# Layer 1 attention of a two-layer model: wider score products, TensorE in a written order, key columns built on VectorE, expert rows fetched earlier

## The chip, the cores and the metric

The kernel runs on one core of one Trainium2 chip. The metric is the device time of one execution in microseconds (us). The time before is the median of three runs, 2395.29 us (2393.6 to 2425.56). The profile comes from one more execution, which took 2390.1 us and whose recorded span, first to last instruction, is 2388.3 us.

## The reference

The input is 32 sequences of 256 tokens with 128 features. Each of two layers adds attention(layernorm(x)) * silu(ffn(layernorm(x))) to x. Layer 0 is a product-of-scores attention with a mixture of eight experts. The change touches layer 1 alone: its attention, and the place where the results of its eight experts are fetched and weighted. Cut to that:

```python
def _strided_allowed(S):                      # STRIDE = 4, LOCAL = 8
    return (j % STRIDE == 0) | (jnp.abs(i - j) <= LOCAL)
...
q, k, v = x @ q_w, x @ k_w, x @ v_w           # 16 heads of 8
q = q * jax.nn.sigmoid(unity_scale)
scores = jnp.einsum('bhqd,bhkd->bhqk', q, k) / jnp.sqrt(D)
scores = jnp.where(_strided_allowed(S), scores, -jnp.inf)
out = jnp.einsum('bhqk,bhkd->bhqd', jax.nn.softmax(scores, axis=-1), v)
return out.reshape(B, S, H) @ o_w + o_b
...
# FFN: top-2 of 8 experts, a slot per token and choice, capacity limited
gathered = out[idx_k, loc_c]
y = jnp.einsum('tk,tkd->td', gates_k * valid, gathered)
```

## The kernel before, in words

The program runs in this order: layer 0, then layer 1's attention for the first half of the tokens (stage A), layer 1's experts (stage M), and layer 1's attention for the second half together with the combination of expert rows for all tokens (stage B). The 8192 tokens lie in 16 blocks of 512, and a block holds two sequences, so stages A and B have 16 sequences each.

**Attention.** A query may see every fourth key and the keys up to 8 places away. So for each block of 64 queries 124 key columns are picked: 64 strided ones and 60 near ones. Two blocks of 64 queries make a stack of 128 partitions; a sequence has two stacks. `prepare` makes one sequence ready: it transposes the normalised rows (`apst`), copies them to `axT`, gathers the key columns into `axk` (the strided ones on VectorE, L779; the near ones in four copies on GpSimd, L781), and multiplies for q, k and v (`apsq`, `apsk`, `apsv`). To keep the four heads that share 32 partitions apart, q is written four times into `aqm`, each time scaled by a mask that leaves one head (L788). The values go to `ava`, with a column of ones that GpSimd sets (L802).

`scores` takes two of the four groups of heads of one stack. Each group has one bank of PSUM (tag `psc`, four banks). A product with the identity first writes the mask of forbidden keys (L813), then 16 products of 32 rows by 64 columns and 124 keys add the scores (L821). VectorE takes the maximum (L828) and subtracts it (L829), ScalarE takes the exponential (L830). `values` transposes four heads (`apsT`, L835), ScalarE copies them to `apT` (L837), and 8 products per group (L842) give the weighted values, with the sum of the weights as a ninth column. `project` divides (L849, L851), transposes (`apso`), multiplies by the output weights (`apsf`) and adds the bias (L861).

The order on each engine comes from a list scheduler that works from its own estimate of times; engines work their queue in that order. `all` writes the rough order: the scores of one stack between the values of the stack before and the `prepare` of the next sequence.

**Moving rows.** In stage A the loop also sends rows to their expert slots: after each stack four indirect DMAs from GpSimd (L157, 128 in all). `pace` lets three start, then a small memset on GpSimd (`breath`, L141) waits for all three to land. Stage M reads these slots only when all have landed. In stage B `combine` fetches the two expert rows of each token of a block with eight indirect DMAs (L1022, 128 in all, paced in the same way), weights and adds them on VectorE (L1033, L1034), takes SiLU on ScalarE (L1036), multiplies by the attention (L1037) and adds x (L1038).

Of the kernel before, what the change touches and what calls it, by code (L numbers as in the profile page):

```python
# [11 lines left out]
F32 = mybir.dt.float32  # L12
# [8 lines left out]
P = 128  # L21
# [12 lines left out]
GROUP0 = (0, 14, 30, 44)  # L34
# [21 lines left out]
def model_kernel(ctx: ExitStack, tc: tile.TileContext, a: dict, out: bass.AP):  # L56
# [56 lines left out]
    qscale = const.tile([P, 4], F32, name="qscale")  # L113
# [106 lines left out]
    with ExitStack() as c0:  # L220
# [479 lines left out]
        us = w0.tile([P, 1], F32, name="us")  # L700
        nc.sync.dma_start(us, a["unity"].partition_broadcast(P))
        nc.scalar.activation(us, us, AF.Sigmoid)
        nc.vector.tensor_scalar(us, us, D ** -0.5, None, ALU.mult)
        nc.vector.tensor_scalar(qscale, hmask, us, None, ALU.mult)
# [49 lines left out]
    class Attention:  # L754

        def __init__(self, c, name, pairs):
            self.ak = c.enter_context(tc.tile_pool(name=f"ak{name}", bufs=2))
            self.pa = c.enter_context(tc.tile_pool(name=f"pa{name}", bufs=2, space=PSUM))  # L760
            self.pa1 = c.enter_context(tc.tile_pool(name=f"pb{name}", bufs=1, space=PSUM))
            self.seqs = [(p, b, dst) for p, dst in pairs for b in range(2)]
            self.steps = self.all()

        def pm(self, name):
            return self.pa1.tile([P, 512], F32, tag="pm", name=name)

        def prepare(self, p, b):
            ak = self.ak
            t0 = p * TT + 2 * b  # L770
            pst = self.pm("apst")
            for i in range(2):
                nc.tensor.transpose(pst[:, i * P : (i + 1) * P], xn[:, t0 + i, :], ident)
            xT = ak.tile([P, S], F32, tag="axT", name="axT")
            nc.scalar.copy(xT, pst[:, :S])

            xk = ak.tile([P, NQB, NK], F32, tag="axk", name="axk")
            grp = xT.rearrange("p (n f) -> p n f", f=4)
            nc.vector.tensor_copy(xk[:, :, 0:QB], bc(grp[:, :, 0], 1, NQB))  # L779
            for i in range(NQB):  # L780
                nc.gpsimd.tensor_copy(xk[:, i, QB:NK].rearrange("p (n f) -> p n f", f=3),  # L781
                                      grp[:, GROUP0[i] : GROUP0[i] + 20, 1:4])
            yield
            psq = self.pm("apsq")
            nc.tensor.matmul(psq[:, :S], lhsT=wqkvo[:, 0, :], rhs=xT, start=True, stop=True)  # L785
            qm = ak.tile([P, 4, S], F32, tag="aqm", name="aqm")
            for j in range(4):
                nc.scalar.activation(qm[:, j, :], psq[:, :S], AF.Copy, scale=qscale[:, j : j + 1])  # L788
            yield
            psk = self.pm("apsk")  # L790
            nc.tensor.matmul(psk[:, : NQB * NK], lhsT=wqkvo[:, 1, :],  # L791
                             rhs=xk.rearrange("p i k -> p (i k)"), start=True, stop=True)
            kT = ak.tile([P, NQB, NK], F32, tag="akT", name="akT")
            nc.scalar.copy(kT.rearrange("p i k -> p (i k)"), psk[:, : NQB * NK])
            yield
            psv = self.pm("apsv")
            for i in range(NQB):
                nc.tensor.matmul(psv[:NK, i * P : (i + 1) * P], lhsT=xk[:, i, :], rhs=wqkvo[:, 2, :],  # L798
                                 start=True, stop=True)

            va = ak.tile([P, NQB, NH, D + 1], F32, tag="ava", name="ava")
            nc.gpsimd.memset(va[:NK, :, :, D : D + 1], 1.0)  # L802
            for i in range(NQB):
                nc.vector.tensor_copy(va[:NK, i, :, 0:D],
                                      psv[:NK, i * P : (i + 1) * P].rearrange("k (h d) -> k h d", d=D))
            self.ready = qm, kT, va

        def scores(self, qm, kT, st, g, pr):

            views = []  # L810
            for w in range(2):
                sc = self.pa.tile([P, 512], F32, tag="psc", name="apsc", bufs=4)[:, : 4 * NK]
                nc.tensor.matmul(sc, lhsT=identb, rhs=keymask[:, st].rearrange("p j k -> p (j k)"),  # L813
                                 start=True, stop=False)
                views.append(sc)
            for u in range(2):
                i = 2 * st + u
                for j in range(4):
                    for w in range(2):
                        r = slice(32 * (g + w), 32 * (g + w) + 32)  # L820
                        nc.tensor.matmul(views[w][u * QB : (u + 1) * QB, j * NK : (j + 1) * NK],  # L821
                                         lhsT=qm[r, j, i * QB : (i + 1) * QB], rhs=kT[r, i, :],
                                         start=False, stop=(j == 3))
            for w in range(2):
                sv = views[w].rearrange("p (j k) -> p j k", j=4)
                to = pr[:, 4 * (g + w) : 4 * (g + w) + 4, :]
# [5 lines left out]
        def values(self, va, st, g, pr, avv):  # L832
            psT = self.pa.tile([P, 4, P], F32, tag="psT", name="apsT")
# [4 lines left out]
            yield  # L838
# [7 lines left out]
        def project(self, avv, dst):  # L846
# [6 lines left out]
            yield  # L853
            pso = self.pm("apso")
            nc.tensor.transpose(pso[:, :P], o, ident)  # L855
            oT = ak.tile([P, P], F32, tag="aoT", name="aoT")
            nc.scalar.copy(oT, pso[:, :P])
            yield
            psf = self.pm("apsf")
            nc.tensor.matmul(psf[:, :P], lhsT=oT, rhs=wqkvo[:, 3, :], start=True, stop=True)  # L860
            nc.vector.tensor_tensor(dst, psf[:, :P], ob, ALU.add)  # L861

        def stack_values(self, va, st, pr, dst):
            av = self.pa1.tile([P, 512], F32, tag="pav", name="apav")
            avv = av[:, : NH * (D + 1)].rearrange("p (h d) -> p h d", d=D + 1)
            for g in range(4):
                yield from self.values(va, st, g, pr, avv)
            yield from self.project(avv, dst)

        def all(self):  # L870

            for _ in self.prepare(*self.seqs[0][:2]):
                pass
            last = iter(())
            for n, (p, b, dst) in enumerate(self.seqs):
                qm, kT, va = self.ready
                if dst is None:
                    dst = self.late[p]
                ahead = iter(())
                for st in range(2):  # L880
                    pr = self.ak.tile([P, NH, NK], F32, tag="apr", name="apr")
                    if st and n + 1 < len(self.seqs):
                        ahead = self.prepare(*self.seqs[n + 1][:2])
                    for g in (0, 2):
                        self.scores(qm, kT, st, g, pr)
                        for _ in range(3):
                            next(last, None)
                            next(ahead, None)
                    for _ in last:
                        next(ahead, None)  # L890
                    for _ in ahead:
                        pass
                    last = self.stack_values(va, st, pr, dst[:, 2 * b + st, :])
                    yield
            for _ in last:
                pass
# [51 lines left out]
    with ExitStack() as ca:  # L948
# [11 lines left out]
        for _ in att.steps:  # L960
            dispatch1(4)
# [53 lines left out]
    with ExitStack() as cb:  # L1015
        bk = cb.enter_context(tc.tile_pool(name="bk", bufs=3))

        def combine(p, s):
# [10 lines left out]
            nc.sync.dma_start(x, x1[p])  # L1029
            y = bk.tile([P, TT, P], F32, tag="yc", name="yc")  # L1030
# [5 lines left out]
            nc.scalar.activation(y, y, AF.Silu)  # L1036
            nc.vector.tensor_tensor(y, y, s, ALU.mult)  # L1037
            nc.vector.tensor_tensor(y, y, x, ALU.add)  # L1038
            nc.sync.dma_start(outv[:, p * TT : (p + 1) * TT, :], y)

        late = range(NEARLY, NP)
        att = Attention(cb, "b", [(p, None) for p in late])
        att.late = {}
        steps = att.steps
        early = list(range(NEARLY))
        held = None
        for p in late:
            att.late[p] = bk.tile([P, TT, P], F32, tag="s1", name="s1")
            for _ in range(4):
                next(steps)  # L1050
            if early:
                q = early.pop(0)
                combine(q, sres[:, q * TT : (q + 1) * TT, :])
            if held is not None:
                combine(held, att.late[held])
            held = p
        for _ in steps:
            pass
        combine(held, att.late[held])


def _layout(i):
# [32 lines left out]
    for b in range(NQB):  # L1095
        keys = np.concatenate([
            np.arange(0, S, 4),
            (4 * (GROUP0[b] + np.arange(20))[:, None] + np.arange(1, 4)[None, :]).ravel(),
        ])
        query = b * QB + np.arange(QB)  # L1100
        allowed = (keys[None, :] % 4 == 0) | (np.abs(query[:, None] - keys[None, :]) <= 8)
        u = b % 2
# [48 lines left out]
```

## Time and profile before

| | us |
|---|---|
| median of three runs | 2395.29 |
| profiled execution | 2390.1 |
| its span | 2388.3 |
| first L781 copy of stage A | 1256.4 |
| first and last L157 row sent | 1286.1, 1538.5 |
| first transpose of stage M (L975) | 1697.1 |
| first and last L1022 row fetched | 1941.7, 2219.4 |

The last four rows, and every time of day in this document, count from the start of the span. Per engine the whole span holds 2153.5 us of matmuls on TensorE (90%), 1191.4 us on VectorE (50%), 990.7 us on ScalarE (41%) and 703.3 us on GpSimd (29%). Those are averages over stages with different limits; the change touches the span from 1255 us to 1697 us and from 1942 us to its end.

The L781 copies mark the sequences. In stage A they start at 1256.4, 1284.5, 1320.7, 1353.8, 1382.8, 1411.9, 1442.1, 1471.1, 1501.2, 1533.8 us and then at 1555.3, 1576.8, 1598.0, 1619.2, 1640.5, 1661.7 us. In stage B they start at 1942.7, 1957.6, 2001.6, 2030.9, 2068.8, 2104.1, 2141.8, 2170.9, 2197.1, 2220.4 us and then at 2238.7, 2261.4, 2287.1, 2307.7, 2328.6, 2349.9 us.

### The profile page before, as it was taken

To read this page: it belongs to the slowest core of one execution; us is meant where nothing else is said; L and a number is where in the kernel's file an instruction comes from. 1 tells how busy PE (TensorE), PEld (TensorE's weight loads), DVE (VectorE), ACT (ScalarE), POOL (GpSimd) and SP (SyncE) were. 2 spreads that over 40 slices of the span, in tenths; PEclk is the share of its full clock that TensorE was granted. 3 is DMA by queue.
4 is the path that set the end of the run, shared out by engine and by line. 5 is a ranking of instruction groups with operands and counts; after the bars stand their busy time and mean duration, and the time that the engine had idled before them with its cause. 6 is when DMAs were issued, how large, how long until landed. Compare 5 with 4: busy or idle time off the path is not lost. (4 is left out here: it accounts for less than half of the span.)

```text
span 2388.3 us, 51723 instructions
## 1 busy us (share of the span) xinstructions
PE 2153.5 (90%) x21618; PEld 1639.4 (69%) x21618; DVE 1191.4 (50%) x2610; ACT 990.7 (41%) x2041; POOL 703.3 (29%) x965
## 2 busy tenths in 40 slices
PE   6999999799999986866978888799999989989998
PEld 4776777588888864544756666577677767767776
DVE  6667666322222245755855444356433336445765
ACT  5523333244343333644742444355311125455654
POOL 0005555122222235555102555400000025444100
PEclk9989999899999987878986888799999977578999
DMA  8502111255454422222112111000122112121100
GB/s 260 178 8 75 43 44 34 85 172 154 149 173 153 148 99 76 80 74 70 44 43 96 33 37 35 25 2 2 55 73 72 64 53 58 50 56 46 36 6 11
DMA packets 131481, 177.19 MB, mean 74 GB/s; under 512 B 16304, under 2 KB 94659, under 8 KB 131248
## 3 DMA queue, kind: packets, MB, share of 16 engines
q1 hardware_dynamic: 103056, 96.57, 12.5%
q0 software_dynamic: 26752, 76.03, 10.7%
q8 instruction: 171, 2.80, 0.5%
q10 hardware_dynamic: 1440, 1.27, 0.2%
q14 instruction: 62, 0.51, 0.1%
HBM read 104.78 MB, written 69.21 MB: 73 GB/s over the span
## 5 line engine op out<-in xcount | busy, mean ns | idle before, releaser
L456 PE MATMUL pp<-qk 64*128 64x128 f32 x2048 | 210.8, 310 | 102.1 <-DVE pat L458 54.2
L441 ACT COPY qk<-ptr 128x512 f32<-128x512 f32 x256 | 149.2, 585 | 352.7 <-PE y L468 268.9
L456 PEld LDWEIGHTS pp<-qk 64*128 64x128 f32 x2048 | 148.9, 193 | 174.1 <-issue 124.8
L821 PE MATMUL apsc<-akT,aqm 32*64 32x124 f32 x4096 | 265.3, 293 | 0.0
L828 DVE TENSOR_REDUCE amx<-apsc 128x4 f32<-128x496 f32 x256 | 163.3, 669 | 190.5 <-PE apsc L821 190.4
L821 PEld LDWEIGHTS apsc<-akT,aqm 32*64 32x64 f32 x4096 | 206.8, 143 | 53.6 <-issue 46.8
L458 DVE TENSOR_TENSOR pat<-pp,dmask 128x512 f32<-128x512 f32 x256 | 175.5, 685 | 128.3 <-PE pp L456 127.0
L837 ACT COPY apT<-apsT 124x512 f32<-124x512 f32 x256 | 146.5, 587 | 177.8 <-PE apsT L835 176.6
L157 POOL DMA_INDIRECT disp<-xn,slot x128 | 136.6, 1067 | 222.3 <-DVE state L431 172.9
L835 PE MATMUL apsT<-ident,apr 128*124 128x128 f32 x1024 | 198.0, 308 | 0.0
L842 PEld LDWEIGHTS apav<-ava,apT 124*64 124x64 f32 x4096 | 152.1, 147 | 66.7 <-issue 29.3
L842 PE MATMUL apav<-ava,apT 124*64 124x9 f32 x4096 | 175.2, 212 | 4.9 <-ACT apT L837 3.0
L439 PE MATMUL ptr<-ident,feat 128*128 128x128 f32 x1024 | 171.0, 285 | 2.6 <-DVE feat L421 2.3
L607 DVE TENSOR_TENSOR od<-edn,wt 128x256 f32<-128x256 f32 x72 | 30.6, 425 | 285.2 <-PE edn L603 285.2
L596 ACT ACTIVATE ha<-eup,wt 128x256 f32<-128x256 f32 x288 | 119.2, 471 | 127.4 <-PE eup L591 124.6
L830 ACT ACTIVATE apr<-apr 128x496 f32<-128x496 f32 x256 | 152.8, 619 | 37.3 <-DVE apr L829 35.7
L829 DVE TENSOR_TENSOR apr<-apsc,amx 128x496 f32<-128x496 f32 x256 | 162.3, 665 | 0.6
L562 POOL DMA_INDIRECT wt<-in_wexp,wrow x72 | 69.0, 959 | 294.1 <-DVE xdT L584 261.3
L622 POOL DMA_INDIRECT rows<-moe,slot x128 | 134.3, 1049 | 65.5 <-issue 29.6
L439 PEld LDWEIGHTS ptr<-ident,feat 128*128 128x128 f32 x1024 | 120.1, 145 | 45.3 <-issue 38.2
L835 PEld LDWEIGHTS apsT<-ident,apr 128*124 128x124 f32 x1024 | 126.7, 152 | 32.2 <-issue 26.5
L802 POOL MEMSET ava<- 124x64 f32 x32 | 6.9, 223 | 478.6 <-DMA moe<-od 278.3
(211 smaller groups left out, 3937.5 us busy)
## 6 DMA issues: line engine op xcount, KB each, us to landing
disp<-zero SPq DMA_DIRECT2D x17, 1024.0 KB, 8.2
xd<-disp SPq DMA_DIRECT2D x72, 128.0 KB, 2.0
moe<-od SPq DMA_DIRECT2D x72, 128.0 KB, 2.0
x<-in_x SPq DMA_DIRECT2D x32, 256.0 KB, 3.3
part<-so SPq DMA_DIRECT2D x16, 512.0 KB, 2.9
soin<-part SPq DMA_DIRECT2D x16, 512.0 KB, 3.8
xd<-disp SPq DMA_DIRECT2D x32, 256.0 KB, 2.6
moe<-od SPq DMA_DIRECT2D x32, 256.0 KB, 2.0
```

Source lines behind the costliest of these rows:

```text
L157: ins = pace(lambda: nc.gpsimd.indirect_dma_start(out=self.dst[:, :], out_offset=bass.IndirectOffsetOnAxis(ap=idx, axis=0), in_=rows, in_o ...
L439: nc.tensor.transpose(pst[:, 2 * n + c], seq.feat[c][:, n, m * P : (m + 1) * P], ident)
L441: nc.scalar.copy(qk, pst)
L456: nc.tensor.matmul(psp[:, w, c], lhsT=qk[r, 2 + c], rhs=qk[r, c], start=True, stop=True)
L458: nc.vector.tensor_tensor(pat, psp, bc(bc(dmask, 1, 2), 1, 2), ALU.mult)
L821: nc.tensor.matmul(views[w][u * QB : (u + 1) * QB, j * NK : (j + 1) * NK], lhsT=qm[r, j, i * QB : (i + 1) * QB], rhs=kT[r, i, :], start=Fa ...
L828: nc.vector.tensor_reduce(mx, sv, AX.X, ALU.max)
L829: nc.vector.tensor_tensor(to, sv, bc(mx, 2, NK), ALU.subtract)
L830: nc.scalar.activation(to, to, AF.Exp)
L835: nc.tensor.transpose(psT[:NK, j, :], pr[:, 4 * g + j, :], ident)
L837: nc.scalar.copy(pT[:NK], psT[:NK])
L842: nc.tensor.matmul(avv[u * QB : (u + 1) * QB, h, :], lhsT=pT[:NK, j, u * QB : (u + 1) * QB], rhs=va[:NK, 2 * st + u, h, :], start=True, st ...
```

## The change

Layers 0 and the experts are left as they are. In layer 1's attention and in `combine`:

- The mask of a head moves from q to k. `qT` is one scaled copy; `kb` holds the keys four times, each with one head's rows left (two copies on ScalarE, two on VectorE). One product of 32 by 64 and 496 columns then gives four heads: eight products a stack in place of 32, and `scores` takes all four groups at once.
- The near keys become a regular window (20 groups of three, from 8 places before the block on), read with one strided VectorE copy from an `axT` that has zeros at both ends. Two fixed `axT` and two fixed `ava` are cleared once for each stage by GpSimd. The strided key columns are no longer copied: k and v are multiplied from `axT` directly.
- In stages A and B TensorE's instructions keep the order in which they are written; `stack` writes it. The other engines keep the list scheduler.
- The small PSUM tiles (`apst`, `apsq`, `apsk`, `apsv`, `apsT`, `apso`, `apsf`) share three banks; before, `apsT` had two and the others one.
- `combine` becomes a generator in three parts: fetch, weight and SiLU, multiply and store. A plan puts them at different stacks.

```diff
         def prepare(self, n):
...
-            xk = ak.tile([P, NQB, NK], F32, tag="axk", name="axk")
-            grp = xT.rearrange("p (n f) -> p n f", f=4)
-            nc.vector.tensor_copy(xk[:, :, 0:QB], bc(grp[:, :, 0], 1, NQB))
+            xT = self.xTs[n % 2]
+            nc.scalar.copy(xT[:, EDGE : EDGE + S], pst[:, :S])
+            strided = xT[:, EDGE : EDGE + S : 4]
+            xw = ak.tile([P, NQB, NK - QB], F32, tag="axw", name="axw")
+            nc.vector.tensor_copy(xw.rearrange("p i (n f) -> p i n f", f=3),
+                                  bass.AP(xT.tensor, xT[:, 1:].offset,
+                                          [xT[:, :].ap[0], [QB, NQB], [4, WG], [1, 3]]))
...
-            for j in range(4):
-                nc.scalar.activation(qm[:, j, :], psq[:, :S], AF.Copy, scale=qscale[:, j : j + 1])
+            nc.scalar.activation(qT, psq[:, :S], AF.Copy, scale=qscale)
...
+            nc.tensor.matmul(psk[:, :, :QB], lhsT=wqkvo[:, 1, :], rhs=bc(strided, 1, NQB),
+                             start=True, stop=True)
+            nc.tensor.matmul(psk[:, :, QB:], lhsT=wqkvo[:, 1, :], rhs=xw, start=True, stop=True)
+            kb = ak.tile([P, NQB, 4, NK], F32, tag="akb", name="akb")
+            for j in (0, 2):
+                nc.scalar.activation(kb[:, :, j, :], psk, AF.Copy, scale=hmask[:, j : j + 1])
+                nc.vector.tensor_scalar(kb[:, :, j + 1, :], psk, hmask[:, j + 1 : j + 2], None, ALU.mult)
...
-                nc.gpsimd.tensor_copy(xk[:, i, QB:NK].rearrange("p (n f) -> p n f", f=3),
-                                      grp[:, GROUP0[i] : GROUP0[i] + 20, 1:4])
...
         def scores(self, qT, kb, st, pr):
...
             for u in range(2):
                 i = 2 * st + u
-                for j in range(4):
-                    for w in range(2):
-                        r = slice(32 * (g + w), 32 * (g + w) + 32)
-                        nc.tensor.matmul(views[w][u * QB : (u + 1) * QB, j * NK : (j + 1) * NK],
-                                         lhsT=qm[r, j, i * QB : (i + 1) * QB], rhs=kT[r, i, :],
-                                         start=False, stop=(j == 3))
+                for g in range(4):
+                    r = slice(32 * g, 32 * g + 32)
+                    nc.tensor.matmul(views[g][u * QB : (u + 1) * QB, :],
+                                     lhsT=qT[r, i * QB : (i + 1) * QB],
+                                     rhs=kb[r, i].rearrange("p j k -> p (j k)"),
+                                     start=False, stop=True)
...
+        def stack(self, front, back, st, ahead, owed):
...
+            pT = {g: self.turn(g, pr) for g in range(2)}
+            if front is not None:
+                self.scores(*front)
+            between = ((ahead,), (owed,), (ahead,), (owed,)) if st == 0 else                 ((ahead,), (), (owed,), (owed, ahead))
+            for g in range(4):
+                self.values(va, sb, g, pT.pop(g), avv)
+                if g < 2:
+                    pT[g + 2] = self.turn(g + 2, pr)
+                for one in between[g]:
+                    next(one, None)
...
-        for _ in att.steps:
-            dispatch1(4)
+        with tc.manual_schedule(engines={mybir.EngineType.PE}):
+            for _ in att.steps:
+                dispatch1(4)
...
+        for n, p in enumerate(range(NEARLY, NP)):
+            plan += [(4 * n + t, p) for t in (2, 5, 6)]
+        for q in range(NEARLY):
+            plan += [(4 * q + t, q) for t in (0, 3, 3)]
```

## The prediction, made before the changed kernel ran

> **What bounds the kernel now.** I read the page first, then the busy time by stretch, the waits, and two stretches of the timeline.
>
> ```profile
> PE 2153.5 (90%) x21618; PEld 1639.4 (69%) x21618; DVE 1191.4 (50%) x2610; ACT 990.7 (41%) x2041; POOL 703.3 (29%) x965
> ...
> PEclk9989999899999987878986888799999977578999
> ```
>
> TensorE looks like the bound at 90%, but its clock is not granted in full in the slices of the two attention stages. The stretches say why (length, then busy us of TensorE, its weight loads, VectorE, ScalarE and GpSimd, then clock, DMA share, GB/s):
>
> ```profile
> 1286.00:1541.00 255.00, 206.43 (x2679) 158.89 (x2681) 108.99 (x234) 101.86 (x208) 137.65 (x211) 0.82 0.11 34
> 1560.00:1690.00 130.00, 128.97 (x1956) 101.45 (x1954) 75.94 (x164) 70.91 (x146) 6.10 (x25) 1.00 0.01 2
> ...
> 1942.00:2220.00 278.00, 259.61 (x2738) 195.26 (x2738) 144.88 (x360) 138.23 (x244) 138.16 (x214) 0.71 0.19 53
> 2220.00:2388.00 168.00, 158.30 (x2313) 122.08 (x2311) 103.18 (x232) 94.81 (x185) 11.66 (x35) 0.98 0.06 17
> ```
>
> While GpSimd moves rows the clock is 0.82 and 0.71, and a sequence takes 31.2 us in stage A (L781 at 1284.5 to 1533.8, eight of them) and 30.9 us in stage B (1942.7 to 2220.4, nine). When the rows are done it takes 21.2 and 21.9 us, TensorE is busy 99% and the clock is 1.00. GpSimd's timeline and TensorE's at the same place show the link:
>
> ```profile
> 1468.12 0.10 POOL L141 MEMSET breath<- 128x1 f32 x1 [1.41 <-DMA disp<-xn,sidx]
> 1468.85 0.97 POOL L157 DMA_INDIRECT disp<-xn,sidx  x1 [0.63 <-POOL breath L141]
> 1470.12 0.98 POOL L157 DMA_INDIRECT disp<-xn,sidx  x1 [0.30 <-issue]
> 1471.10 0.75 POOL L781 COPY axk<-axT 128x60 f32<-128x60 f32 x4
> ...
> 1466.57 0.33 PE L835 MATMUL apsT<-ident,apr 128*124 128x128 f32 x1
> 1471.90 2.02 PE L791 MATMUL apsk<-axk,wqkvo 128*128 128x496 f32 x2 [5.01 <-POOL axk L781]
> ```
>
> The near keys stand in GpSimd's queue behind rows that wait for their landing. TensorE idles 5 us, and its next product (2.02 us; 1.00 us in the dense stretch) runs at half clock.
>
> **The change, part by part.**
>
> *Key columns off GpSimd.* With nothing of the attention in that queue, eight sequences of stage A lose up to 31.2 - 21.2 = 10 us each. The rows alone take 5.7 us for three (L141 at 1468.12 to the next at 1474.42, less the 0.6 us that L781 adds), so 43 groups end at 1286 + 245 = 1531, ahead of the attention's new end below. GpSimd's new memsets, 12 of about 0.2 us, half of them (stage B's) behind the second row sent, cost the rows 1 to 3 us: nothing, under that cover.
>
> *The score product.* TensorE's work is read from starts:
>
> ```profile
> 1589.05 0.37 PE L813 MATMUL apsc<-keymask,identb 128*128 128x496 bf16 x1
> 1589.36 1.55 PE L821 MATMUL apsc<-akT,aqm 32*64 32x124 f32 x32
> 1590.83 0.64 PE L842 MATMUL apav<-ava,apT 124*64 124x9 f32 x16
> 1591.40 0.65 PE L835 MATMUL apsT<-ident,apr 128*124 128x128 f32 x4
> ```
>
> One L785 pass of 256 columns takes 379 ns and one L791 pass of 496 columns 579 ns, so a column costs 0.83 ns and a product has two passes. 124 columns are 0.103 us, so 32 passes one after the other would take 3.3 us; they took 1.55 us. Two groups of rows and two of columns run side by side. A stack has two such blocks, 2.95 us from start to L842. Now it has 16 passes of 0.413 us in eight places of the array. If all eight places work together, with about 60 ns from one product's start to the next (32 loads and passes went out at some 15 ns each), the block takes 7 * 0.06 + 2 * 0.413 + 0.1 = 1.35 us. If only two places work at once it takes 3.3 us. I take 1.35, since L821 already had four places at work. Per stack TensorE then has: mask 4 * 0.21, scores 1.35, L835 16 * 0.107, L842 4 * 0.55, output 0.32, and of the next sequence half of 2.6 us (the extra L798 product, 0.2 us, included): 7.7 us, against 9.2 before. Before, 18.3 us of such work per sequence took 21.2 us; the rest is changes between shapes, which I put at 0.7 us a stack now.
>
> *TensorE's written order.* All four groups of scores now end together, and the next stack's scores need the four banks back. VectorE needs 4.8 us for them (two L828 and two L829 take 2.43 us). In the built order of the changed kernel there are two kinds of step. Light: after the last subtraction come two masks and the block (0.1 + 0.4 + 1.35 + 0.25 = 2.1 us), so VectorE's loop is 6.9 us and TensorE's sum, 7.7 us, decides. Heavy (next k and v): the three shared small banks are taken by k, by v and by `apsf`, so the next transposes wait until VectorE, behind its last subtraction, has done one `kb` copy (0.55 us, as L794) and the bias (0.25); then transposes, a ScalarE copy (0.65) and transposes again through one bank (2.2 us), masks 0.83, block and landing 1.6: 5.35 us, so 10.15 us. What waits behind it is everything of TensorE, and VectorE's other copies hide there. A sequence takes 17.9 us. VectorE's added work (two `kb` copies, wider `ava` copies, about 1.2 us a sequence) and ScalarE's (two `kb` copies for four L788 and L794) are under that cover; without it VectorE's own sum is some 14 us.
>
> *Stage A:* first softmax at 1286 (1282.1 before; it now needs four banks, of which routing holds two until L910 ends), 31 steps of 8.95 us, 9 us for the last values and output, 8 us for a half-clock start as at 1285 to 1305, 2.8 us for the first load of stage M: 1584 in place of 1697.1. **113 us less.**
>
> *Rows fetched ahead.* Fetches go three in 5.9 to 7 us; the 128 of them took 278 us with L781 between, 43 groups of about 6.2 us without. But VectorE's built queue has the weighting of 64 fetched rows ahead of its ninth softmax, and it works in order. Those rows land at 1943 + 64 * 6.2 / 3 = 2075 us, so steps 0 to 8 are paced by rows, 16 us each, and the ninth softmax starts at about 2077; before, the copies of the sequence it belongs to stood at 2068.8. Then 23 steps of 8.95 us, eight blocks that add 2.6 us each (L1033 and L1034, four of 0.29 and four of 0.33 us, less 0.9 us of idle VectorE, and about 1 us for two ScalarE table loads of 1.28 us each), 15 us until the clock recovers, and 14 us of tail (as 2374 to 2388): 2333 in place of 2388.3. **55 us less.**
>
> Sum: 2390.1 - 168 = **2222 us** on the profiled execution's scale; the median shown is 0.2% higher.
>
> **The clock.** Counting each matmul record's columns, passes and share of 128 rows in stretches of 3.41 us, stages A and B keep the full clock when the count reaches 0.40 of what the array could stream, and mostly lose it or fail to regain it below. The dense stretch has 0.57, or 12.0 us of full streaming a sequence; 17.9 us gives 0.67. The page "TensorE: Matmul & The Clock Gate" of the Trainium skill (HAM oscillation) has the clock fall only when TensorE idles for about 3.4 us; this trace differs, with 2030 to 2090 us at 0.58 though TensorE was busy 56.74 of 60 us. By the page the 23 us for half clock would go: 2199.
>
> **Rivals.**
> 1. *Products go out strictly one after the other.* Each then waits for the first pass of the one before: 8 * 0.413 + 0.4 = 3.7 us a block, 2.35 us more a step, 73 and 54 us: 2349. Against it: under such an order L821's 16 products could not have ended in 1.55 us (15 * 0.103 until the last starts, plus its own 0.26 = 1.8). [...] Chance 0.10.
> 2. *Steps are shorter, or VectorE never waits for rows.* TensorE's 16.7 us a sequence: 33 us less; the ninth softmax at 2030: 47 less. 2142 to 2189. For it: rows are asked for earlier. Chance 0.17.
> 3. *Fetching does not run ahead.* Rows pace stage B to their end (2217), then six steps and the tail: 2290. For it: 278 us of fetching now. Chance 0.08.
> 4. *Half clock sticks: slower.* If waits in the heavy step keep the count below 0.40, steps take about 15.3 us (TensorE's sums doubled but for waits): 31 * 6.35 - 8 and 23 * 6.35 - 15 = 320 us more, 2542. It decides from 15 us a step on (6 / 15 = 0.40). For it: stage B's ten-window lows; against it: 0.67. Chance 0.05.
>
> **The numbers.** My case has 0.60. A step wrong by 0.7 us moves 38 us, the row-paced start 15. The range 2150 to 2320 holds my case with these, rival 3 and most of 2. About 2% can be told from no change. Faster by more (under 2342): 0.60 + 0.17 + 0.08 and 0.03 of rival 1; within 2%: the rest of it, 0.07; slower 0.05.
>
> **What would show it.** GpSimd's rows with nothing between, three in 5.7 us; eight-product blocks of 1.35 us; light and heavy steps of 7.7 and 10.2 us at clock 1.00 from about 1310; VectorE idle for rows until about 2077; stage M's first transpose near 1584. I am wrong if blocks take over 2 us, if the clock stays below 0.9 in stage A, or if stage B's steps are not paced by rows early.

## The result, and the profile after

| | before | after |
|---|---|---|
| median | 2397.5 us of 4 runs (2393.6 to 2425.56) | 2214.8 us of 4 runs (2211.96 to 2215.44) |
| ratio, 95% interval | | 0.9212 (0.9142 to 0.9283) |
| span of the profiled execution | 2388.3 | 2213.7 |
| stage A, first transpose to the first of stage M | 441.8 | 317.8 |
| stage M, to the first row fetched | 244.6 | 245.5 |
| stage B, to the end | 446.6 | 391.9 |

The change is faster by 182.7 us of the medians, 174.6 us of the spans. Stage M starts 120.8 us earlier (stage A is 124.0 us shorter, but starts 3.2 us later), and stage B is 54.7 us shorter. A few runs of one kernel come out some per cent longer at a lower clock, and the times compared here are of the others: so of the kernel before beside e1 to e4, and beside e3b, e7 and e8, one run each counts (2437.5 and 2424.8 us), and e3's profile is of such a longer run (2578.7 us). The page of the profile has TensorE hardly less busy, at 89%, but the slices of stage A (the 25th to the 28th, from 1328 us on) at full clock:

```profile
PE 1963.4 (89%) x18674; PEld 1445.9 (65%) x18674; DVE 1232.4 (56%) x2609; ACT 968.0 (44%) x1977; POOL 662.9 (30%) x817
...
PEclk9989999899999999877979789999999997788889
```

The busy time by stretch, with the columns as before, shows where the clock is whole and where it is not:

```profile
1286.00:1530.00 244.00, 232.24 (x2997) 158.74 (x2997) 187.90 (x366) 147.18 (x297) 127.25 (x173) 0.99 0.12 35
...
1822.00:1953.00 131.00, 89.36 (x867) 58.16 (x867) 79.23 (x183) 65.75 (x107) 65.65 (x87) 0.74 0.22 59
1953.00:2086.00 133.00, 117.03 (x1328) 81.41 (x1327) 98.71 (x214) 82.50 (x149) 62.04 (x83) 0.85 0.20 51
2086.00:2213.00 127.00, 110.98 (x1392) 77.92 (x1384) 92.66 (x195) 74.18 (x141) 0.94 (x1) 0.90 0.07 21
```

Stage A, the first row, now runs at 0.99 while the same rows move. Stage B has two parts: until 1953 us TensorE is busy 68% of the time, and from there 88%. The timeline of TensorE in stage A shows one heavy step, from score block to score block:

```profile
1489.23 1.09 PE L838 MATMUL apsc<-akb,aqT 32*64 32x496 f32 x16
...
1491.31 1.06 PE L803 MATMUL apsk<-axT,wqkvo 128*128 128x256 f32 x2
1492.19 0.59 PE L805 MATMUL apsk<-axw,wqkvo 128*128 128x240 f32 x2
...
1496.77 0.66 PE L853 MATMUL apsT<-ident,apr 128*124 128x128 f32 x4
1498.16 0.66 PE L853 MATMUL apsT<-ident,apr 128*124 128x128 f32 x4 [0.73 <-ACT apT L855]
1498.65 1.00 PE L831 MATMUL apsc<-keymask,identb 128*128 128x496 bf16 x4
1499.58 1.09 PE L838 MATMUL apsc<-akb,aqT 32*64 32x496 f32 x16
```

The block takes 1.09 us, the step 10.35 us, and the only wait in it is 0.73 us for a copy by ScalarE. L805 follows L803 at once: the near keys (`axw`) are no longer waited for. GpSimd's timeline has its rows with nothing between them:

```profile
1469.43 0.10 POOL L142 MEMSET breath<- 128x1 f32 x1 [1.41 <-DMA disp<-xn,sidx]
1470.16 0.98 POOL L158 DMA_INDIRECT disp<-xn,sidx  x1 [0.63 <-POOL breath L142]
1471.45 0.98 POOL L158 DMA_INDIRECT disp<-xn,sidx  x1 [0.31 <-issue]
```

### The profile page after: what moved, and what is told of

The parts are those of the page before. It is cut to its first block, busy times and chain, and to the rows that moved or that the text cites. A ratio compares the mean times of both kernels' runs of the same rounds, so it can differ in the third digit from the quotient of the medians.

```text
span 2213.7 us, 45584 instructions
## 1 busy us (share of the span) xinstructions
PE 1963.4 (89%) x18674; PEld 1445.9 (65%) x18674; DVE 1232.4 (56%) x2609; ACT 968.0 (44%) x1977; POOL 662.9 (30%) x817
## 4 chain that ended last, share of the span: by engine, by line
PE 40%; DMA 5%; POOL 4%; ACT 3%; issue 3%; DVE 1%; POOLq 0%; ACTq 0%; DVEq 0%; SPq 0%
PE apsT L853 6%; PE apav L862 6%; PE mpsd L1027 5%; PE mpsu L1014 5%; PE apsc L838 3%; DMA rows<-moe,slot 3%; PE apsc L831 3%; POOL rows L623 2%; DMA rows<-moe,gidx 2%; PE apsf L873 1%; PE apsv L815 1%; ACT apr L848 1%; PE apsk L803 1%; POOL rows L1055 1%; PE pp L457 1%
## 5 line engine op out<-in xcount | busy, mean ns | idle before, releaser
L1055 POOL DMA_INDIRECT rows<-moe,gidx x128 | 124.5, 973 | 338.8 <-ACT aqT L800 286.5
L862 PEld LDWEIGHTS apav<-ava,apT 124*64 124x64 f32 x4096 | 143.6, 140 | 113.5 <-issue 52.9
L846 DVE TENSOR_REDUCE amx<-apsc 128x4 f32<-128x496 f32 x256 | 159.8, 665 | 75.3 <-PE apsc L838 74.8
L853 PE MATMUL apsT<-ident,apr 128*124 128x128 f32 x1024 | 170.5, 301 | 29.4 <-ACT apT L855 14.6
L862 PE MATMUL apav<-ava,apT 124*64 124x9 f32 x4096 | 167.0, 208 | 22.8 <-ACT apT L855 21.7
L853 PEld LDWEIGHTS apsT<-ident,apr 128*124 128x124 f32 x1024 | 120.3, 149 | 47.5 <-ACT apT L855 19.7
L158 POOL DMA_INDIRECT disp<-xn,sidx x128 | 125.8, 983 | 80.5 <-DVE sidx L958 27.1
L592 PE MATMUL eup<-xdT,wt 128*128 128x256 f32 x576 | 142.3, 389 | 1.8 <-DMA wt<-in_wexp,wrow 1.8
```

Source lines behind the costliest of these rows:

```text
L158: ins = pace(lambda: nc.gpsimd.indirect_dma_start(out=self.dst[:, :], out_offset=bass.IndirectOffsetOnAxis(ap=idx, axis=0), in_=rows, in_o ...
L846: nc.vector.tensor_reduce(mx, sv, AX.X, ALU.max)
L853: nc.tensor.transpose(psT[:NK, j, :], pr[:, 4 * g + j, :], ident)
L862: nc.tensor.matmul(avv[u * QB : (u + 1) * QB, h, :], lhsT=pT[:NK, j, u * QB : (u + 1) * QB], rhs=va[:NK, 2 * st + u, h, :], start=True, st ...
```

## The experiments

They ran on several chips, and the chips differ. On the chip of the runs called c0, e9, e5 and e6 the kernel before took 2380 to 2397 us and the changed kernel repeats its first times. On the three chips of the others the kernel before took 2412 to 2445 us, and while rows move TensorE's results come late there, by 2.5 us in the lines of the last section. On those chips I therefore read mainly the stretch of stage A after the last row (from about 1545 us on), where no such delay is seen, and compare times with the kernel before on the same chip. The times expected for e3b, e4, e7 and e8 were worked out for the first chip, and all four came out longer.

| run | time, us | stage A | a sequence of A with no rows moving | stage B |
|---|---|---|---|---|
| before | 2397.5 | 441.8 | 21.2 | 446.6 |
| changed | 2214.8 | 317.8 | 17.9 | 391.9 |
| c0 changed, again | 2206.4 | 317.3 | 17.9 | 392.0 |
| e9 near keys off GpSimd, burst | 2367.5 | 396.8 | 23.1 | 478.2 |
| e5 key copies on ScalarE | 2299.4 | 377.4 | 21.5 and 22.9 | 424.7 |
| e6 no table change | 2169.0 | 317.6 | 17.9 | 349.0 |
| other chips: e1 near keys off GpSimd alone | 2427.1 | 454.7 | 21.2 | 470.6 |
| e2 near keys back on GpSimd | 2356.2 | 441.0 | 17.9 | 415.3 |
| e4 scheduler's order | 2357.5 | 423.4 | 19.9 | 435.9 |
| e3 four pieces in a row | 2498.9 (2578.7 profiled) | 510.7 | 24.9 | 564.2 |
| e3b pieces in turn | 2354.7 | 414.9 | 18.9 | 428.3 |
| e7 VectorE in written order | 2256.1 | 372.9 | 17.9 | 388.7 |
| e8 SiLU by exponential | 2263.5 | 359.1 | 17.1 | 395.4 |
| e10 SiLU by tanh | 2239.4 | 359.8 | 17.1 | 376.9 |

**c0: the changed kernel again.** No edit.

> The changed kernel as it is, beside the other runs on one chip, since the kernel before took 2437 to 2500 us beside the first four experiments and 2394 to 2426 us beside the changed kernel. If its gain is of the kernel and not of a chip: steps of 7.5 and 10.35 us at full clock in stage A, and 2210 to 2225 us. Rival, half clock catches it on some chips as it caught the parts run alone: sequences of 25 us or more in stage A and over 2300 us.

2206.4 us against 2389.2 on the same chip, ratio 0.9226 (0.918 to 0.9272); steps of 7.5 and 10.35 us. The gain is the kernel's.

**e1: near keys off GpSimd alone.**

```diff
-                nc.gpsimd.tensor_copy(xk[:, i, QB:NK].rearrange("p (n f) -> p n f", f=3),
+                nc.vector.tensor_copy(xk[:, i, QB:NK].rearrange("p (n f) -> p n f", f=3),
...
-            nc.gpsimd.memset(va[:NK, :, :, D : D + 1], 1.0)
+            nc.vector.memset(va[:NK, :, :, D : D + 1], 1.0)
```

> The kernel before, with one part of the change alone: the copies of the near keys and the memset beside the values' columns go from GpSimd to VectorE; the four score products for each head, the scheduler's order of TensorE and the place of the row fetches stay. My theory: the near-key copy that waited behind paced row sends was what kept a sequence of stage A at 31 us instead of 21 to 22 us while rows moved (8 sequences of 16 fall in that time, the others already ran at 21 to 22 us). So stage A becomes about 80 us shorter, the granted clock in it goes to about 1.0, stage B gains 10 to 40 us, and the time is 2270 to 2310 us. Rival, the wide score product is what brought the gain: the sequences stay near 30 us and the time stays within 30 us of 2395.

A miss: 2424 to 2430 us, against 2437.5 on that chip. The stretches with and without rows, columns as above:

```profile
1300.00:1530.00 230.00, 219.86 (x2316) 168.30 (x2316) 96.02 (x233) 85.74 (x175) 119.15 (x157) 0.70 0.11 34
1545.00:1690.00 145.00, 144.41 (x2126) 112.37 (x2124) 87.94 (x215) 77.94 (x159) 0.00 (x0) 0.99 0.01 2
```

The 5 us waits for GpSimd are gone and TensorE is busy 96% by its records, yet a sequence takes some 32 us at clock 0.70 while rows move, and 21.2 us after. The late results of this chip are in that stretch (28 starts of VectorE and ScalarE over 0.3 us late), so the run does not say what the part is worth on the chip of the prediction. It does say that taking the wait away is not enough where the streamed count stays low for another reason: counted as in the prediction, its half-clock windows hold 0.25 to 0.50, with the middle one at 0.35.

**e2: near keys back on GpSimd.**

```diff
-            nc.vector.tensor_copy(xw.rearrange("p i (n f) -> p i n f", f=3),
+            nc.gpsimd.tensor_copy(xw.rearrange("p i (n f) -> p i n f", f=3),
```

> The changed kernel, with the copy of the near keys back on GpSimd and all else as changed. My theory: the copy queues behind paced row sends again, so a sequence of stage A takes 28 to 31 us instead of 17.9 us while rows move, stage A is 90 to 120 us longer, the granted clock in it falls to 0.6 to 0.8, and the time is 2300 to 2360 us. Rival, with the rest of the change the copy is no longer waited for (TensorE's written order puts other products ahead of the score products): stage A is less than 20 us longer, and the time stays below 2240 us.

2354.7 to 2357.7 us. Stage A is 441.0 us, and a sequence is back at 17.9 us once the rows are sent. The first row is from the table of TensorE's waits between 1286 and 1530 us (total us, times, longest); the others are TensorE's and GpSimd's timeline around one of them:

```profile
PE apsk L805 <- POOL axw L792: 59.4, 6, 15.1
```

```profile
1450.61 1.06 PE L803 MATMUL apsk<-axT,wqkvo 128*128 128x256 f32 x2
1462.66 1.17 PE L805 MATMUL apsk<-axw,wqkvo 128*128 128x240 f32 x2 [10.98 <-POOL axw L792]
```

```profile
1460.50 0.10 POOL L142 MEMSET breath<- 128x1 f32 x1 [1.40 <-DMA disp<-xn,sidx]
1461.23 0.98 POOL L158 DMA_INDIRECT disp<-xn,sidx  x1 [0.63 <-POOL breath L142]
1462.20 0.40 POOL L792 COPY axw<-axT 128x240 f32<-128x240 f32 x1
```

A copy of 0.40 us costs TensorE 11 us, since GpSimd comes to it only behind rows that wait for their landing, and the product after it, 1.17 us against 0.59, runs at half clock. With TensorE's order fixed, all its later work waits too. This settles the link: the wait and the half clock return with the one copy. Its six waits come to 59.4 us, and stage A is 68 us longer than e7's, whose stage A has the changed kernel's instructions, on another chip with late results.

**e3 and e3b: the width of the score product.** Both cut each product of 496 columns into four of 124; e3 gives all four to one place in a row, e3b goes round the four groups of rows:

```diff
 e3
                 for g in range(4):
                     r = slice(32 * g, 32 * g + 32)
+                    for j in range(4):
...
 e3b
+                for j in range(4):
+                    for g in range(4):
+                        r = slice(32 * g, 32 * g + 32)
```

> The changed kernel, with each score product of 496 columns cut into four products of 124 columns to the same place of the array: 32 products of a stack (64 passes) instead of 8 (16 passes), the same columns in all. My theory: the block of a stack is then set by the launches of passes and no longer by columns shared over eight places, and takes 1.9 to 2.5 us instead of 1.09 us; a step of 7.55 or 10.35 us becomes about 1 us longer, stage A 25 to 35 us and stage B up to 25 us longer, time 2240 to 2275 us. Rival one, products start strictly in order and only neighbours overlap: the block takes over 3.5 us and the time goes above 2300 us. Rival two, the width does not matter, since the step is set by the chain through VectorE and ScalarE: the time stays within 8 us of 2215.

> The changed kernel with the score product in four pieces of 124 columns, as in the run where a stack's block took 4.42 us, but the pieces go to the four groups of rows in turn, where they went four in a row to one place of the array. Both blocks measured so far come to 68 or 69 ns a pass (16 passes of 496 columns in 1.09 us, 64 of 124 columns in 4.42 us), the block of the kernel before to 48 ns (32 passes of 124 columns in 1.55 us, two places in turn). Theory one, a pass waits for the one before it at its own place and places overlap: with four places in turn the block takes 1.6 to 2.5 us, a sequence of stage A 19 to 21 us at full clock, and the time is 2240 to 2300 us. Theory two, each pass has a price of its own whatever place it goes to: 3.1 to 4.4 us a block again, a sequence of 23 us or more with stretches at half clock, and 2400 us or more.

In the stretch without rows, e3's block, then e3b's:

```profile
1637.39 4.42 PE L839 MATMUL apsc<-akb,aqT 32*64 32x124 f32 x64
```

```profile
1564.32 1.58 PE L839 MATMUL apsc<-akb,aqT 32*64 32x124 f32 x64
```

The same 64 passes take 4.42 or 1.58 us by their order alone, and a sequence 24.9 (the two at full clock) or 18.9 us. The starts of single passes say how: at another place the next pass starts 6 to 7 ns later, at the same place 106 ns later (124 columns). So my expectation for e3 (1.9 to 2.5 us) was wrong, its rival one had the size, and theory one of e3b is right. In turn, the pieces cost 1.0 us a sequence more than the wide product. Width is therefore worth little where the places are visited in turn; "one product for four heads" brings 0.5 us a block over that.

**e4: the scheduler's order of TensorE.**

```diff
-        with tc.manual_schedule(engines={mybir.EngineType.PE}):
-            for _ in att.steps:
-                dispatch1(4)
+        for _ in att.steps:
+            dispatch1(4)
```

(the same in stage B).

> The changed kernel without its written order of TensorE: the scheduler places the products as it did before, all else as changed. My theory: most of the gain of stage A came from the near keys leaving GpSimd, and the written order only fills the wait for the softmax; a sequence of stage A takes 19 to 22 us instead of 17.9 us, stage A is 20 to 60 us longer, and the time is 2235 to 2290 us. Rival one, the order is what the gain rests on: sequences over 25 us and a time above 2310 us. Rival two, the scheduler finds an order as good: within 10 us of 2215.

2355.7 to 2359.2 us, beyond the band of the first theory; but 19.9 us a sequence without rows, as it has it. The written order is worth 2.0 us a sequence there. Stage A as a whole is 50 us longer than e7's; how much of that is the order, and how much the late results on top of it, is not told apart.

**e9: a burst against half clock.** e1, and in each sequence 11 more mask products in a row, whose result is overwritten:

```diff
+                for _ in range(11 if st == 0 and g == 0 and w == 0 else 0):
+                    nc.tensor.matmul(sc, lhsT=identb, rhs=keymask[:, st].rearrange("p j k -> p (j k)"),
+                                     start=True, stop=True)
```

> The kernel with the near keys off GpSimd alone (2427 us), with 11 needless mask products in a row added once in each sequence. They are 0.21 us each at full clock, 2.3 us a sequence, and their results are overwritten. Theory: in that kernel TensorE stays at half clock while rows move, since what it streams in a window of 3.41 us (0.25 to 0.40 of the array) stays below 0.40 even when it is busy all the time; the burst gives one window in each sequence above 0.40, so the clock comes back once a sequence. Sequences of stage A then take 24 to 27 us in place of 28 to 31 us while rows move, the granted clock from 1286 to 1530 us goes from 0.71 to over 0.85, stage B gets shorter too, and the time falls to 2350 to 2410 us though work was added. Rival, the clock does not go by what is streamed: every sequence becomes 2.3 to 4.6 us longer, 32 times, and the time goes to 2500 to 2570 us.

2367.5 us, ratio 0.9884 (0.9772 to 0.9997), too near 1 to be told from no change. Its stretch with rows:

```profile
1286.00:1530.00 244.00, 243.16 (x3430) 180.73 (x3429) 136.26 (x339) 124.13 (x254) 123.05 (x162) 1.00 0.11 35
```

With rows or without, a sequence takes 23.1 us at full clock; before, 31 and 21.2. The time lies in the expected band, but the test of the burst is inconclusive: on this chip no result comes late, so nothing is known to pull the clock down without the burst, and stage B (478 us, clock 0.81) is 32 us longer than before, about what its 16 bursts add. What the run does show is the near-key part, together with the burst, on the prediction's kind of chip: the effect of the rows on a sequence of stage A vanishes, and stage A falls from 441.8 to 396.8 us although 16 bursts of some 1.9 us were added. Less those, about 75 us (an estimate: 45 + 16 * 1.9). The part was not run without the burst on such a chip, so whether the burst helped is open.

**e5: key copies on ScalarE.**

```diff
             for j in (0, 2):
                 nc.scalar.activation(kb[:, :, j, :], psk, AF.Copy, scale=hmask[:, j : j + 1])
-                nc.vector.tensor_scalar(kb[:, :, j + 1, :], psk, hmask[:, j + 1 : j + 2], None, ALU.mult)
+                nc.scalar.activation(kb[:, :, j + 1, :], psk, AF.Copy, scale=hmask[:, j + 1 : j + 2])
```

> The changed kernel with all four copies of the masked keys on ScalarE, where VectorE did two. My theory of the heavy step: TensorE's next transposes wait for a bank that VectorE frees only behind its last subtraction and one copy of the keys; so without those copies on VectorE the heavy step goes from 10.35 us to 8 to 9.5 us, the light step stays at 7.5, stage A is 15 to 35 us shorter, and the time is 2170 to 2205 us. Rival, ScalarE (133 us busy in 220 us of stage A, and two copies of about 0.65 us more a sequence) then holds the exponentials or the transposed copies back: the heavy step stays or grows, and the time is 2215 us or more.

2299.4 us, ratio 0.9615 (0.9555 to 0.9675): heavy steps of 13.9 to 15.4 us. From its timeline:

```profile
1417.10 0.60 ACT L854 COPY apT<-apsT 124x512 f32<-124x512 f32 x1
...
1417.75 1.03 PE L861 MATMUL apav<-ava,apT 124*64 124x9 f32 x16 [2.97 <-ACT apT L854]
1418.71 0.80 PE L872 MATMUL apsf<-wqkvo,aoT 128*128 128x128 f32 x2
```

The copy of the transposed probabilities now stands behind key copies and exponentials, TensorE waits 3 us, and its next products are at half clock (L872 0.80 us against 0.49). The rival holds: with VectorE's copies gone, nothing got shorter. Since ScalarE held TensorE up in their place, the run alone does not say what those copies cost; the changed kernel's own trace does (next section).

**e6: no table change.** Leaves out SiLU; an exponential stands in its place.

```diff
-            nc.scalar.activation(y, y, AF.Silu)
+            nc.scalar.activation(y, y, AF.Exp)
```

> The changed kernel with an exponential in the place of SiLU where the rows are combined (SiLU is left out). So ScalarE needs no change between the two function tables in stage B. Theory: the heavy steps of stage B (14.2 to 15.3 us against 10.35 us in stage A) are long because two table loads of 1.28 us and the SiLU of 0.63 us hold up the exponentials and the transposed copies, and TensorE then falls to half clock for two windows. Heavy steps of stage B go to 11 to 12.5 us, the granted clock in it from 0.83 to over 0.9, and the time is 2175 to 2200 us. Rival, VectorE's weighting and adding of rows (2.6 us a block) is what makes them long: heavy steps stay at 13 us or more and the time stays above 2205 us.

2169.0 us, ratio 0.9069 (0.9022 to 0.9117). Stage B is 43 us shorter, at clock 0.90 against 0.83; heavy steps after the ninth softmax take 10.3 to 12.4 us in place of 14.1 to 15.1, light ones 7.5. In the changed kernel ScalarE's groups and TensorE's waits, from 1950 to 2086 us, had:

```profile
L1070 ACT ACT_TABLE_LOAD x6 | 7.7, 1283 | 0.1
L848 ACT ACT_TABLE_LOAD x6 | 7.7, 1283 | 0.1
```

```profile
PE apav L862 <- ACT apT L855: 8.4, 5, 1.7
PE apsf L873 <- ACT aoT L870: 6.8, 6, 2.5
```

and without the loads TensorE's waits from 1950 to 2072 us are the 0.7 us ones of stage A:

```profile
PE apsT L853 <- ACT apT L855: 5.1, 7, 0.7
PE apsf L873 <- ACT aoT L870: 1.5, 3, 0.5
```

The rival (VectorE's work on the rows) falls: that work is still there. So is an activation of the same length where SiLU was (631 ns for 630), so it is the two loads of each block that hold TensorE up.

**e7: VectorE, too, in written order in stage B.**

```diff
-            plan += [(4 * q + t, q) for t in (0, 3, 3)]
+            plan += [(4 * q + t, q) for t in (0, 3, 4)]
...
-        with tc.manual_schedule(engines={mybir.EngineType.PE}):
+        with tc.manual_schedule(engines={mybir.EngineType.PE, mybir.EngineType.DVE}):
```

> The changed kernel with VectorE, too, in the written order in stage B (as TensorE is), and the last part of an early block's combination one stack later. My theory: the first eight steps of stage B take 13 us on average (against 9 in stage A) because VectorE's built queue has the weighting of 64 fetched rows ahead of the ninth softmax. In the written order that weighting comes when the rows have landed: the ninth softmax starts 75 to 90 us after the first row fetch, in place of 131 us, the later steps wait for rows at most as long as the last rows need (264 us from the first fetch), and stage B is 20 to 45 us shorter, 2160 to 2190 us. Rival, the rows pace stage B as a whole: what is gained at the start is waited for later, since the last weighting still comes 264 us after the first fetch: within 10 us of 2206.

2251 to 2261 us, on a chip with late results, so the time says little. The ninth softmax starts 96 us after the first fetch, in place of 131: the wait for rows was the queue's order. But then steps take 12 us, and fetching lasts 351 us: GpSimd now waits for VectorE to free the three buffers of rows (59.9 us in all; in the changed kernel 3.1 us),

```profile
POOL rows L1055 <- DVE yc L1068: 59.9, 8, 9.0
```

and stage B, 388.7 us, is about as long as the changed kernel's elsewhere. Most of what is gained early is paid later; how much of that is the chip's late results is not told apart.

**e8 and e10: without the table change, with SiLU.** e8 makes SiLU as y / (1 + exp(-y)), e10 as y/2 * (1 + tanh(y/2)); both put the mask products between the two first groups of transposes. e10:

```diff
-            pT = {g: self.turn(g, pr) for g in range(2)}
+            pT = {0: self.turn(0, pr)}
+            views = self.masks(front[2]) if front is not None else None
+            pT[1] = self.turn(1, pr)
...
-            nc.scalar.activation(y, y, AF.Silu)
+            nc.scalar.activation(en, y, AF.Tanh, scale=0.5)
+            nc.vector.scalar_tensor_tensor(y, en, 1.0, y, ALU.add, ALU.mult)
...
-            nc.vector.tensor_tensor(y, y, s, ALU.mult)
+            nc.vector.scalar_tensor_tensor(y, y, 0.5, s, ALU.mult, ALU.mult)
```

> The changed kernel with two edits. SiLU of the combined rows is made as y / (1 + exp(-y)), the exponential on ScalarE, the sum, the reciprocal and the product on VectorE, so that no table is changed in stage B and the output stays the reference's. And the four mask products go between the two first groups of transposes, where TensorE waits 0.73 us in each heavy step. Theory: stage B keeps most of what it gained without SiLU (349 us against 392), since VectorE is busy 170 of 220 us in stage A and has room for some 2 us more a block; the wait in the heavy step goes, 16 times 0.7 us in stage A: 2150 to 2175 us. Rivals: VectorE's queue then holds the softmax up in stage B (360 to 390 us, 2180 to 2205 us); the mask products only move the wait elsewhere (stage A stays at 317 us).

> The changed kernel with SiLU of the combined rows made as y/2 * (1 + tanh(y/2)): the tanh on ScalarE, whose table is then the exponential's and is not changed in stage B, and one wider product on VectorE; and with the four mask products between the two first groups of transposes. Both as the run with the exponential and a reciprocal, without its reciprocal, which took VectorE 3.35 us a block (53.5 us in stage B). Theory: where ScalarE and VectorE do not start late while rows move (as beside the changed kernel's own runs), stage A takes 300 to 306 us (17.0 us a sequence, as measured after the last row in that run), stage B 335 to 355 us, and the time is 2140 to 2165 us, 0.893 to 0.907 of the kernel before; where they start late it is 2210 to 2250 us. Rival, the mask products gain nothing while rows move: stage A 314 to 318 us and 2160 to 2180 us.

e8: 2255.6 to 2271.4 us. Its first rival fits, by one line of VectorE's groups in stage B, though the late results of its chip are in the time too:

```profile
L1079 DVE RECIPROCAL en<-en 128x512 f32<-128x512 f32 x16 | 53.5, 3345 | 0.2
```

e10, without it: 2239.4 us, ratio 0.923 (0.9159 to 0.9301) on its chip, in the band for chips with late results; stage B 376.9 us. In both, a sequence without rows takes 17.1 us in place of 17.9, so the mask products fill the wait. Both beat the kernel before. Whether e10 beats the changed kernel is open: the two never ran on one chip. The changed kernel less e6's gain and 16 * 0.8 us (2206.4 - 37.4 - 13) would be about 2156 us, an estimate that leaves out e10's wider product on VectorE.

## Why the prediction was right or wrong

**Near keys on GpSimd (80 us of the forecast): right.** Rows' effect on a sequence was 10 us before, and it is 0 after, 17.9 us with rows and without. e2 brings it back with one copy; e9, with its burst beside it, takes it away from the kernel before. The mechanism is shown; the 80 us of the part alone are not: e9's 75 us has the burst in it, and e1 gained nothing in stage A on a chip with late results. The rows ended at 1533 us (forecast 1531).

**The score block, 1.35 us: right in kind, 1.09 us in size.** The eight first passes start 7 ns apart and the second ones 466 ns after the first ones, so all eight places do work together; my 60 ns between products was too much. Rival 1 is out, yet it is true within one place: e3 shows its price. The Trainium skill's "strict FIFO, no reordering" ("TensorE: Matmul & The Clock Gate", Packing small matmuls) is said of the order in which matmuls start and end. The block keeps that order product by product, though its passes interleave, the second of the first product after the first of the eighth. The v products do not keep it: L813's product stands ahead of L815's first in the program, and its second pass starts at 1495.97 us, after that of L815's (1495.91).

**Light step 7.7, heavy step 10.15: sizes right (7.55 and 10.35), the reason of the heavy one wrong.** The step that failed is "the next transposes wait until VectorE, behind its last subtraction, has done one `kb` copy (0.55 us, as L794) and the bias (0.25)". In the heavy step shown above VectorE had

```profile
1495.03 0.72 DVE L810 TENSOR_SCALAR akb<-apsk,hmask 128x496 f32<-128x496 f32 x1
1495.86 0.29 DVE L874 TENSOR_TENSOR sres<-apsf,ob 128x128 f32<-128x128 f32 x1
```

so both were done by 1496.15 us, and the transposes start at 1496.77, right behind the v products (L815) and without a wait. TensorE's own work decides: 171.65 us busy in the 179 us of ten sequences (1311.25 to 1490.25 us), 17.2 of 17.9 us, with the 0.73 us behind `apT` the rest. That wait, transposes twice through one bank, I had foreseen. The prediction has TensorE's sum at 16.7 us (its terms, with 0.7 us a stack for changes between shapes, add to 16.8). The heavy step is longer since the k and v products stand in it: TensorE is busy for 9.62 us of it, and for all 7.55 us of the light one. So the close sizes are in part luck: 7.7 was a mean of both kinds of step without the changes between shapes, measured at 8.6, and 10.15 came from a path that was not waited for (whose terms, besides, add to 5.43 and not 5.35 us). e10 shows that the 0.73 us can be filled.

**Stage A, 113 us less: measured 121.** The 8 us for a half-clock start did not come: the full clock is there from 1292 us and stays to 1572, and from the first softmax (1285.4 us; forecast 1286) to stage M there are 291 us in place of 298.

**Ninth softmax paced by rows: right.** It starts 130.9 us after the first fetch (forecast 134). VectorE's weighting just ahead of it waits for a row, and the softmax (L846) follows at 1952.72 us; e7 moves it to 96 us by the queue's order.

```profile
1952.45 0.35 DVE L1068 SCALAR_TENSOR_TENSOR yc<-rows,gate,yc 128x128 f32<-128x128 f32 x1 [1.06 <-DMA rows<-moe,gidx]
```

**The rest of stage B: right in sum, wrong in its terms.** Forecast 256 us from the ninth softmax to the end, measured 261. But I had eight blocks at 2.6 us, about 1.6 of it VectorE's work on rows, and one recovery of 15 us: 36 us. In fact VectorE's work is hidden, and each of eight heavy steps is 4 to 5 us longer than in stage A (14.1 to 15.1 us), 35 us in all, because two table loads hold back ScalarE's copies and the clock then halves for two windows of 3.41 us. e6 takes 35 of the 261 us away. Two errors cancelled, which is luck.

**The clock.** The count of 0.40 held as a rule to read by: 0.42 or more in each window of stage A from 1292 to 1569 us and no half clock; in each heavy step of stage B one window below 0.40 (0.06 to 0.38), and two at half clock behind it. e9 could not test it. In those steps TensorE also idles for 2.4 to 2.8 us, so it is the stretch that the prediction names, at 0.58 though TensorE was busy 56.74 of 60 us, that speaks for the count and against idling alone.

## What to carry to other kernels

A cheap instruction in the queue of an engine that waits for transfers costs what it waits, and half clock after it; move such an instruction before making the bound engine's work smaller. A bound engine that is busy 96% still needs its small waits looked at one by one, and the engine that serves them (ScalarE here) has no room for moved work, even when its total is at 60%. Products that may share the array should go to its places in turn, and a function on ScalarE should be chosen for the table that is already loaded.

## What the runs showed of the hardware

- **Chips differ while rows move.** e7's instructions in stage A are the changed kernel's; it took 372.9 us there, against 317.3 to 317.8 in three executions elsewhere. The delay is on TensorE's side, as its records' modelled ends do not show:

```profile
1315.24 0.49 PE L873 MATMUL apsf<-wqkvo,aoT 128*128 128x128 f32 x2
...
1315.93 0.82 PE L815 MATMUL apsv<-wqkvo,axw 128*60 128x128 f32 x6
...
1318.24 0.29 DVE L874 TENSOR_TENSOR sres<-apsf,ob 128x128 f32<-128x128 f32 x1 [2.74 <-PE apsv L815]
```

L874 needs only L873, which by its record ended at 1315.73. TensorE's semaphore events stand in the trace at 1317.51, 1318.22 and 1318.33 us, and VectorE starts with the second. By the waits that the profile links to TensorE, starts over 0.3 us late (to 1.5 us) number 89 to 128 in each of the eight profiles on three chips, every one within 10 us of the issue of an indirect row DMA, and none in the four profiles on the other chip and the first two. Their cause is open, and with it whether it lies in the chip; no kernel was profiled on chips of both kinds except by e7's unchanged stage A.
- **A reciprocal on VectorE** takes 3345 ns for 512 columns and 253 ns for 16 (e8), some 6.2 ns a column more, against 642 ns for a product of 512.
- **Tanh and the exponential** need no table load between them (none in e10's stage B); the exponential and SiLU need one of 1283 ns each way (30 in the changed kernel's).
